# Layer 1 of a four-layer convolution chain: the negated row maxima reach all partitions by a DRAM write and read

## The chip, the core and the metric

The kernel runs on one core of a Trainium2 chip, in float32. The metric is device microseconds from the start to the end of one execution; the number given for a kernel is the median of its runs. A profile is one execution of its own, taken by the hardware profiler.

## The reference

Four layers follow each other on an input of 4 images x 192 channels x 64 x 64. Layer 0 is a deformable convolution with channel attention and an MLP, layer 2 is windowed attention with an MLP, layer 3 is a dynamic depthwise convolution. The change is in layer 1, a non-local block over all 4096 positions of an image:

```python
g_x = _conv1x1(x, g_w, g_b).reshape(B, O, N)            # O = 96, N = 4096
theta_x = _conv1x1(x, theta_w, theta_b).reshape(B, O, N)
phi_x = _conv1x1(x, phi_w, phi_b).reshape(B, O, N)
f1 = jnp.einsum('bon,bom->bnm', theta_x, phi_x)
f_div_C = jax.nn.softmax(f1, axis=-1)
y = jnp.einsum('bnm,bom->bon', f_div_C, g_x)
return _conv1x1(y.reshape(B, O, H, W), W_w, W_b) + x
```

The softmax of a query runs over all 4096 keys, and its maximum is taken off before the exponential.

## The kernel before

One program handles the four images (b = 0 to 3) in turn: layer 1, layer 2's windows, then the rest of layers 2 and 3. Layer 0 of the next image is spread over them. Its gather (an indirect DMA per tap and unit of 128 pixels into `ring`, blends on ACT and DVE into `row` and `xo`, matmuls `h`) is woven into layer 1 of images 0 to 2: `beside(k + 1)` in `layer1` emits some two and a half taps a step. Each unit of that gather also loads its centre pixels, `ti` (L584), with two DMAs on SP's queue into one of three buffers. Image 3 has no next image, so its layer 1 is alone.

Keys lie on the partitions and queries along the free dimension. `keys` makes `ph` (phi) and `gx` (g, with a column of ones for the softmax's sum). `layer1` goes through 16 chunks of 256 queries (QN), and for each through 8 groups (NG) of 4 x 128 keys (G). A step k is one group of one chunk:

- `load(i)` (L928 to L933): a chunk's x comes by DMA into `xc` (SP's queue, but ACT's for the first two chunks of images 1 and 2; four buffers); a matmul and an ACT copy make theta, `ths`.
- `score(i, g)` (L939 to L946): four score matmuls of 128 keys x 256 queries into PSUM (two buffers), an ACT copy of the 128 x 1024 block to a slot in SBUF, and a DVE maximum into `top`. There are 10 slots in images 0 to 2 and 16 in image 3.
- `negated_max(i)`, once per chunk: two more DVE maxima (L951, L952) bring `top` down to 128 x 256. Two TensorE transposes (`mt`, L955) put queries on the partitions, and a DVE reduction with negation (`nm`, L957) leaves 128 x 2 numbers: query 128 j + p in row p, column j. The next step needs them along the free dimension and the same on every partition. So DVE scales the identity by each column (`dg`, L960), TensorE multiplies that by a matrix of ones (`mb`, L963), and ACT copies the product to SBUF (`mbs`, L965), which is 128 x 256.
- for a step k of the main loop: DVE adds `mbs` to the slot (L1002), ACT takes the exponential (L1003), and TensorE adds the product with `gx` to `y` (L1005). After a chunk's last group, `y` is copied (L1011), and `finish` (L971 to L981) divides by the sum, applies W, adds x, and writes back to DRAM from SP's queue (L981).

A float32 matmul appears in the profile as two matmul records, so the two `mb` matmuls of a chunk are four records.

PSUM tag "a" has one buffer; `th`, `mt`, `mb`, `pd` and `wy` take it in turn. In the program, step k also emits the scores of step k + 10 (images 0 to 2) or k + 16 (image 3), and a chunk's `negated_max` follows its eighth score group. The order on each engine and queue isn't the program's order: a planner (the tile framework's scheduler) places each instruction by its readiness and its place in the program, and puts semaphore waits where one engine needs another or a buffer. The queues of SP, ACT and POOL then issue in that fixed order, and an instruction that waits holds all behind it on its engine.

Of the kernel before, what the change touches and what calls it, by code (L numbers as in the profile page):

```python
# [10 lines left out]
F32 = mybir.dt.float32  # L11
# [39 lines left out]
QN, G, EXTRA = 256, 4, 2  # L51
# [29 lines left out]
def conv_seq_kernel(ctx: ExitStack, tc: tile.TileContext, a, out: bass.AP):  # L81
    nc = tc.nc

    def pool_of(**kw):

        return tc.tile_pool(**({} if kw.get("space") == DRAM else {"reuse_waits": "tile"}), **kw)
# [4 lines left out]
    dram = ctx.enter_context(pool_of(name="tables", bufs=1, space=DRAM))  # L91
# [241 lines left out]

    xn_flat = [dram.tile([C, XNW], F32, tag=f"xnd{i}", name=f"xnd{i}") for i in range(2)]
    x_flat = [dram.tile([C, HW], F32, tag=f"xd{i}", name=f"xd{i}") for i in range(2)]
    xn_drams, x_drams = ([t.rearrange("(k p) n -> p k n", p=P) for t in ts] for ts in (xn_flat, x_flat))

    def variances(pv, sq, mean):
# [559 lines left out]
    def layer1(b, kv, beside):  # L898

        ph, gx = kv  # L900
        with ExitStack() as s:
            keep = s.enter_context(pool_of(name="l1", bufs=1))
            sb = s.enter_context(pool_of(name="l1a", bufs=2))
# [44 lines left out]
            def negated_max(i):  # L948

                top = tops.pop(i)  # L950
                nc.vector.tensor_tensor(top[:, 0:2], top[:, 0:2], top[:, 2:4], ALU.max)  # L951
                nc.vector.tensor_tensor(top[:, 0], top[:, 0], top[:, 1], ALU.max)  # L952
                pt = ps1.tile([128, 2, 128], F32, tag="a", name=f"mt_{b}_{i}")
                for j in range(2):
                    nc.tensor.transpose(pt[:, j, :], top[:, 0, bass.ts(j, 128)], ident)  # L955
                nm = sb.tile([128, 2], F32, tag="nm", name=f"nm_{b}_{i}")
                nc.vector.tensor_reduce(nm, pt, AX.X, ALU.max, negate=True)  # L957
                dg = sb.tile([128, 2, 128], F32, tag="dg", name=f"dg_{b}_{i}")
                for j in range(2):
                    nc.vector.tensor_scalar_mul(dg[:, j, :], ident, nm[:, j : j + 1])  # L960
                pb = ps1.tile([128, 2, 128], F32, tag="a", name=f"mb_{b}_{i}")
                for j in range(2):
                    nc.tensor.matmul(pb[:, j, :], lhsT=ones, rhs=dg[:, j, :], start=True, stop=True)  # L963
                mb = sb.tile([128, QN], F32, tag="mb", name=f"mbs_{b}_{i}")
                nc.scalar.copy(mb, pb.rearrange("p j n -> p (j n)"))  # L965
                return mb

# [18 lines left out]
            def next_scores(k):  # L986
                if k < NQ * NG:
                    i, g = divmod(k, NG)
                    if g == 0:
                        load(i)  # L990
                    score(i, g)
                    if g == NG - 1:
                        mbs[i] = negated_max(i)
# [3 lines left out]
            for k in range(NQ * NG):  # L997
                i, g = divmod(k, NG)
# [878 lines left out]
    with ExitStack() as s:  # L1877
        sb = s.enter_context(pool_of(name="l0first", bufs=1))
# [14 lines left out]
    with ExitStack() as s:  # L1893
        sb, pool = (s.enter_context(pool_of(name=n, bufs=1)) for n in ("norms0", "l0d0"))
# [4 lines left out]
    for b in range(B):  # L1899
        with ExitStack() as s:  # L1900
            sb = s.enter_context(pool_of(name="l1x", bufs=1))
# [36 lines left out]
        held = [oi]  # L1938
# [77 lines left out]
```

## Time and profile before

| | |
|---|---|
| median of 14 runs | 6950.65 us |
| lowest of the runs | 6923.98 us |
| profiled execution: its own time | 6973.63 us |
| profiled execution: span of the trace | 6971.9 us |
| granted TensorE clock, mean | 0.936 |
| busy: PE, PEld | 6270.0 us (90%), 4235.7 us (61%) |
| busy: DVE, ACT, POOL | 4791.0 us (69%), 3705.0 us (53%), 2038.0 us (29%) |
| chain that ended last | PE 60%, DVE 19%, ACT 7%, issue 5%, DMA 3% |

PE is TensorE's matmuls, PEld its weight loads (they overlap), DVE the vector engine, ACT the scalar engine, POOL GpSimd, SP the engine whose queue issues most DMAs. In the page, a line such as PE or DVE with 40 digits gives the busy share in tenths of 40 equal slices of the span, some 174 us each; DMA is the mean busy share of the 16 DMA engines. The chain is followed back from the last instruction through what released each step. In a timeline line stand the start in us, the duration in us, the engine, the source line, the operation, the tiles written and read, and the shapes; "x4" are four instructions of one kind merged, and brackets give the engine's idle time ahead and what ended it. SPq marks the issue of a DMA. In the windows view each engine has its busy us and its number of instructions in a stretch, then come the mean granted clock, the DMA engines' busy share and GB/s.

Layer 1's loops lie at about 915 to 1590, 2550 to 3230, 4190 to 4870 and 5735 to 6235 us.

### The profile page before, as it was taken

What the parts mean: (1) busy time and instruction counts of PE and PEld (TensorE: products, weight loads), DVE (VectorE), ACT (ScalarE), POOL (GpSimd) and SP (SyncE); (2) the same over time, 40 slices, a digit from 0 to 9 for tenths busy, and PEclk for the clock granted to TensorE, in tenths of its full rate; (3) what the DMA queues carried; (4) which work ended last, traced back from release to release, by engine and by line L of the source; (5) the groups of instructions that cost most, each with busy time, mean ns of one, the idle gap of its engine ahead of it and who ended that gap; (6) DMA issues with size and microseconds to landing.
All of it is one profiled execution on the core that took longest, in us unless ns stands there. A gap on an engine that the chain in (4) does not pass through costs nothing.

```text
span 6971.9 us, 116124 instructions
## 1 busy us (share of the span) xinstructions
PE 6270.0 (90%) x45392; PEld 4235.7 (61%) x45392; DVE 4791.0 (69%) x7011; ACT 3705.0 (53%) x6134; POOL 2038.0 (29%) x2276
## 2 busy tenths in 40 slices
PE   8787999999988899999988899999998889999876
PEld 4445578886643467887654457878564357776432
DVE  3654179985577758995676848987567767765656
ACT  3664268874544357884544337876444425545331
POOL 3663057642200036761210016763210000012100
PEclk8789989999989999999989999999999989999988
DMA  6784246651000166662010056764100010010000
GB/s 189 259 289 147 78 157 220 210 166 34 23 26 14 60 188 198 216 210 79 11 33 22 17 154 191 225 202 138 35 24 29 14 52 10 14 36 12 7 3 20
DMA packets 330499, 699.39 MB, mean 100 GB/s; under 512 B 60077, under 2 KB 217181, under 8 KB 329182
## 3 DMA queue, kind: packets, MB, share of 16 engines
q0 software_dynamic: 92736, 455.22, 20.0%
q1 hardware_dynamic: 236382, 235.95, 11.8%
q8 instruction: 358, 5.87, 0.3%
q14 instruction: 191, 1.56, 0.1%
q10 hardware_dynamic: 832, 0.79, 0.0%
HBM read 611.25 MB, written 78.87 MB: 99 GB/s over the span
## 4 chain that ended last, share of the span: by engine, by line
PE 60%; DVE 19%; ACT 7%; issue 5%; DMA 3%; another core or an unknown queue 1%; POOL 1%; SPq 0%; DVEq 0%; POOLq 0%; ACTq 0%
PE s L939 10%; PE y L1005 9%; PE h L608 6%; PE v L1170 2%; PE qk L1095 2%; DVE ha L1347 2%; PE h L1547 2%; PE qk L1096 2%; DVE ga L1347 2%; PE po L496 2%; PE t L1178 1%; PE h L821 1%; DVE top L946 1%; DVE row L597 1%; PE zm L1558 1%
## 5 line engine op out<-in xcount | busy, mean ns | idle before, releaser
L590 POOL DMA_INDIRECT ring<-table,idx x1152 | 1608.9, 1397 | 1178.8 <-issue 268.4
L939 PE MATMUL s<-ths,ph 96*128 96x256 f32 x4096 | 994.6, 390 | 21.6 <-ACT ths L933 12.8
L939 PEld LDWEIGHTS s<-ths,ph 96*128 96x128 f32 x4096 | 794.1, 195 | 165.4 <-ACT ths L933 21.4
L596 ACT ACTIVATE row<-ring,pos 128x384 f32<-128x384 f32 x1152 | 674.9, 609 | 219.3 <-DVE xo L601 122.4
L597 DVE SCALAR_TENSOR_TENSOR row<-ring,fr,row 128x384 f32<-128x384 f32 x1152 | 674.8, 612 | 100.5 <-ACT row L596 69.0
L1005 PE MATMUL y<-sc,gx 128*97 128x256 f32 x3008 | 721.6, 380 | 0.0
L1005 PEld LDWEIGHTS y<-sc,gx 128*97 128x97 f32 x3008 | 489.5, 164 | 126.9 <-issue 2.3
L600 ACT ACTIVATE xo<-row,pos 128x192 f32<-128x192 f32 x1152 | 489.1, 449 | 132.3 <-remote 50.9
L601 DVE SCALAR_TENSOR_TENSOR xo<-row,fr,xo 128x192 f32<-128x192 f32 x1152 | 449.6, 411 | 103.5 <-ACT xo L600 67.3
L941 ACT COPY sc<-s 128x1024 f32<-128x1024 f32 x376 | 378.0, 1005 | 193.1 <-PE s L939 168.3
L1002 DVE TENSOR_TENSOR sc<-sc,mbs 128x1024 f32<-128x1024 f32 x376 | 447.1, 1218 | 37.9 <-issue 20.7
L608 PE MATMUL h<-ti,xo 128*128 128x192 f32 x2304 | 456.6, 333 | 5.6 <-DVE xo L601 5.2
L946 DVE TENSOR_TENSOR top<-top,sc 128x1024 f32<-128x1024 f32 x282 | 344.5, 1222 | 163.2 <-ACT sc L941 133.3
L608 PEld LDWEIGHTS h<-ti,xo 128*128 128x128 f32 x2304 | 399.3, 194 | 42.3 <-DVE xo L601 12.0
L1003 ACT ACTIVATE sc<-sc 128x1024 f32<-128x1024 f32 x376 | 393.1, 1054 | 32.1 <-DVE sc L1002 25.2
L1154 DVE TENSOR_REDUCE es<-ex 128x6 f32<-128x384 f32 x264 | 133.3, 546 | 361.7 <-ACT ex L1150 361.7
L608 PE MATMUL h<-kept,xo 128*128 128x192 f32 x960 | 254.5, 403 | 112.9 <-DVE xo L601 71.0
L1588 POOL COPY gate<-gate 128x192 f32<-128x192 f32 x12 | 4.2, 351 | 1116.2 <-ACT gate L1581 1116.2
L608 PEld LDWEIGHTS h<-kept,xo 128*128 128x128 f32 x960 | 185.1, 226 | 202.9 <-DVE xo L601 104.8
L1347 DVE SCALAR_TENSOR_TENSOR ga<-gate,v,ga 128x1024 f32<-128x1024 f32 x234 | 299.7, 1281 | 7.2
L1005 PE MATMUL y<-se,gx 128*97 128x256 f32 x1088 | 260.4, 379 | 0.5 <-ACT yn L1011 0.5
L1552 ACT ACTIVATE z<-h,bias_fc1T 128x512 f32<-128x512 f32 x192 | 118.0, 687 | 227.2 <-PE h L1549 226.9
(392 smaller groups left out, 11573.3 us busy)
## 6 DMA issues: line engine op xcount, KB each, us to landing
ti<-table SPq DMA_DIRECT2D x768, 48.0 KB
ring<-table,idx POOLq DMA_INDIRECT x1152
xnd<-xn SPq DMA_DIRECT2D x4, 3270.0 KB
xi<-in_x_dram SPq DMA_DIRECT2D x32, 384.0 KB
xk<-xd SPq DMA_DIRECT2D x32, 384.0 KB
xd<-xc SPq DMA_DIRECT2D x64, 192.0 KB
table<-tt SPq DMA_DIRECT2D x32, 384.0 KB
xc<-xd SPq DMA_DIRECT2D x60, 192.0 KB
```

Source lines behind the costliest of these rows:

```text
L590: nc.gpsimd.indirect_dma_start(out=gt.rearrange("p q r c -> p (q r c)"), out_offset=None, in_=corners, in_offset=bass.IndirectOffsetOnAxis ...
L596: nc.scalar.activation(row, gt[:, 0], AF.Copy, scale=pos[:, t, 9 + tap : 10 + tap])
L597: nc.vector.scalar_tensor_tensor(row, gt[:, 1], fr[:, t, 9 + tap : 10 + tap], row, ALU.mult, ALU.add)
L600: nc.scalar.activation(xo[:, j, :], row[:, 0, :], AF.Copy, scale=pos[:, t, tap : tap + 1])
L601: nc.vector.scalar_tensor_tensor(xo[:, j, :], row[:, 1, :], fr[:, t, tap : tap + 1], xo[:, j, :], ALU.mult, ALU.add)
L608: nc.tensor.matmul(acc[m // 2][:, bass.ts(m % 2, C)], lhsT=xo.rearrange("p j c -> p (j c)")[:, bass.ts(m, 128)], rhs=tt, start=t == 0 and ...
L939: nc.tensor.matmul(p[:, t, :], lhsT=ph[:, bass.ts(G * g + t, 128)], rhs=ths[i], start=True, stop=True)
L946: nc.vector.tensor_tensor(tops[i], tops[i], to, ALU.max)
L1002: nc.vector.tensor_tensor(ex, ex, mbs[i].unsqueeze(1).to_broadcast([128, G, QN]), ALU.add)
L1003: nc.scalar.activation(ex, ex, AF.Exp)
L1005: nc.tensor.matmul(py, lhsT=gx[:, G * g + t, :], rhs=ex[:, t, :], start=g == 0 and t == 0, stop=g == NG - 1 and t == G - 1,)
L1347: nc.vector.scalar_tensor_tensor(acc[:, b], src(tap, b), w[:, tap : tap + 1], acc[:, b], ALU.mult, ALU.add)
```

## The change

For every chunk but the first of an image (60 of 64), `nm` is written to a DRAM tile of 256 numbers from SP's queue, in the order of the queries, and a second DMA on the same queue reads those 256 numbers into `mb` on all 128 partitions. Two DRAM tiles alternate. `dg`, the two matmuls with `ones` and ACT's copy remain for the first chunk of each image; `dg` has one buffer instead of two. Nothing else is touched.

```diff
+    max_dram = [dram.tile([QN], F32, tag=f"maxd{i}", name=f"maxd{i}") for i in range(2)]
...
                 nm = sb.tile([128, 2], F32, tag="nm", name=f"nm_{b}_{i}")
                 nc.vector.tensor_reduce(nm, pt, AX.X, ALU.max, negate=True)
-                dg = sb.tile([128, 2, 128], F32, tag="dg", name=f"dg_{b}_{i}")
+                mb = sb.tile([128, QN], F32, tag="mb", name=f"mbs_{b}_{i}")
+                if i > 0:
+                    held = max_dram[i % 2]
+                    nc.sync.dma_start(out=held.rearrange("(j p) -> p j", p=128), in_=nm)
+                    nc.sync.dma_start(out=mb, in_=held.unsqueeze(0).to_broadcast([128, QN]))
+                    return mb
+                dg = sb.tile([128, 2, 128], F32, tag="dg", name=f"dg_{b}_{i}", bufs=1)
                 for j in range(2):
                     nc.vector.tensor_scalar_mul(dg[:, j, :], ident, nm[:, j : j + 1])
                 pb = ps1.tile([128, 2, 128], F32, tag="a", name=f"mb_{b}_{i}")
                 for j in range(2):
                     nc.tensor.matmul(pb[:, j, :], lhsT=ones, rhs=dg[:, j, :], start=True, stop=True)
-                mb = sb.tile([128, QN], F32, tag="mb", name=f"mbs_{b}_{i}")
                 nc.scalar.copy(mb, pb.rearrange("p j n -> p (j n)"))
                 return mb
```

## The prediction

> **What bounds the kernel now.** I read the page first: its slices, then the chain of work that ended last.
>
> ```profile
> PE   8787999999988899999988899999998889999876
> DVE  3654179985577758995676848987567767765656
> DMA  6784246651000166662010056764100010010000
> PE s L939 10%; PE y L1005 9%; PE h L608 6%; PE v L1170 2%; PE qk L1095 2%; DVE ha L1347 2%; PE h L1547 2%; PE qk L1096 2%; DVE ga L1347 2%; PE po L496 2%; PE t L1178 1%; PE h L821 1%; DVE top L946 1%; DVE row L597 1%; PE zm L1558 1%
> ```
>
> Layer 1's loop fills slices 7 to 9, 16 to 18 and 25 to 27 (images 0 to 2, with the next image's gather beside it; DMA shows 5 to 7 there) and 34 to 36 (image 3, alone; DMA 0 or 1). PE shows 8 and 9 in them, DVE 8 and 9 in the first three. The two costliest lines of the chain, L939 and L1005, are its score and output matmuls. So I read single chunks of queries in the windows view: an undisturbed one of image 2, one of image 2 with a stall, one of image 3.
>
> ```profile
> core 0: us, PE busy (x) PEld busy (x) DVE busy (x) ACT busy (x) POOL busy (x), PEclk, DMA share, GB/s
> 4449.26:4490.49 41.23, 41.23 (x206) 34.53 (x205) 39.24 (x65) 35.14 (x62) 33.70 (x21) 1.00 0.73 229
> 4618.00:4667.00 49.00, 45.84 (x205) 37.40 (x204) 39.59 (x64) 35.63 (x60) 30.11 (x23) 0.90 0.64 204
> 5854.50:5885.70 31.20, 31.05 (x146) 24.61 (x144) 22.36 (x25) 16.67 (x19) 0.00 (x0) 1.00 0.04 13
> ```
>
> In the undisturbed chunk PE is busy for 41.23 of 41.23 us, at full clock, with DVE at 39.24. In image 3 it is 31.05 of 31.20. PE is the bound of both; DVE comes close in images 0 to 2. The stalled chunk takes 49 us at a mean clock of 0.90: an idle PE is paid twice. Next the tile view of `mb`, who waited for it:
>
> ```profile
>   ACT mbs L965: 92.2, 22
>   DVE sc L1002: 17.0, 14
>   PEld th L931: 14.3, 6
> ```
>
> Then the timeline across one undisturbed chunk boundary (chunk 5 of image 2), which shows what the maxima gate:
>
> ```profile
> 4409.62 0.42 DVE L957 TENSOR_REDUCE nm<-mt 128x2 f32<-128x256 f32 x1
> 4410.28 0.47 DVE L960 TENSOR_SCALAR dg<-ident,nm 128x128 f32<-128x128 f32 x2
> 4410.72 0.68 PE L963 MATMUL mb<-dg,ones 128*128 128x128 f32 x4
> 4411.64 0.35 ACT L965 COPY mbs<-mb 128x256 f32<-128x256 f32 x1
> 4412.39 2.35 DVE L1002 TENSOR_TENSOR sc<-sc,mbs 128x1024 f32<-128x1024 f32 x2
> 4413.86 1.04 ACT L1003 ACTIVATE sc<-sc 128x1024 f32<-128x1024 f32 x1
> 4414.01 3.72 PE L939 MATMUL s<-ths,ph 96*128 96x256 f32 x16
> 4417.57 1.89 PE L1005 MATMUL y<-sc,gx 128*97 128x256 f32 x8
> ```
>
> `nm` ends at 4410.04, `mbs` at 4411.99, the first addition starts 0.40 us later, and the chunk's first output matmuls (L1005 on `sc`) start at 4417.57. By program order `mbs` is wanted three steps after it is made; in the trace it is wanted at once: at each `nm` the additions of all earlier chunks are done (I counted 8n additions before the n-th `nm` in every image), and PE has at most one step (8 matmuls) of the previous chunk left in images 0 to 2. What PE has to do across the boundary is that rest, `th`, two score groups (3.72 us) and some gather matmuls. They fill it just to 4417.57.
>
> **Removed, on 60 of the 64 chunks.** PE: four matmuls `mb`. In the boundary shown the next output matmul follows 0.51 us after `mb`'s start, in image 3 it is 0.44 us, which is what PE gets back: 45 x 0.51 + 15 x 0.44 = 30 us. DVE: two `dg`, 0.47 us a chunk, 28 us; ACT: one copy of 0.37 us, 22 us. DVE and ACT are not the bound, so I count only PE's 30 us. The PSUM slot "a" is now free after `nm` and not after `mbs`, so `th` can start about 2 us earlier; the order of PE's work changes by it, its amount doesn't. I price it at nothing; PE being full across the boundary hides it.
>
> **Added.** Two DMAs on SP's queue, the second waiting for the first to land. The trace has no such pair for 1 KB, but it has one of the same kind: the write of x back (L981) and the load (L928) that waits for that write. Quiet (image 3), then beside the gather (image 1):
>
> ```profile
> 5870.17 0.30 SPq L981 DMA_DIRECT2D xd<-xc  x1
> 5872.30 0.30 SPq L928 DMA_DIRECT2D xc<-xd  x1
> ```
>
> ```profile
> 2795.13 0.31 SPq L981 DMA_DIRECT2D xd<-xc  x1
> 2797.68 2.36 SPq L584 DMA_DIRECT2D ti<-table  x4
> 2800.09 0.58 SPq L928 DMA_DIRECT2D xc<-xd  x1
> ```
>
> Quiet, the dependent read is issued 2.13 us after the write. Beside the gather it is 4.96 us; the other pairs that I looked at in image 1 have 3.83 to 4.73. The last packet of the quiet read ends 1.87 us after its issue by the trace's packets, beside the gather at 2.96 to 3.41 (medians by image). Both rows move 192 packets of 1 KB, the new read 128 of 1 KB, the new write 256 of 4 bytes, if each element is a packet. Packets of 4 bytes take 9 ns and of 1 KB 46 ns here, so the data is nothing: 16 x 9 and 8 x 46 ns on each engine. From `nm`'s end to `mbs` ready the bounds are 2.13 + 1.87 = 4.0 us and 4.96 + 3.41 = 8.4 us, against 1.69 (image 3) and 1.95 us (image 2) now. For image 3 I take 4.0, it has no gather. For images 0 to 2 the DMA engines are busy 0.73 of the time, so the loaded rows are nearer; the pair is smaller than they are, and I take 6.4.
>
> The Trainium skill, DMA: Bandwidth & Descriptors, section Anatomy of one DMA, speaks against the change: it puts a fixed cost of about 2.0 us on each DMA, most of it the receipt of the write. By that rule a pair would be 4 us in every image, and the sum would be the first rival's. The quiet row agrees (2.13 us); the loaded one doesn't.
>
> **Images 0 to 2.** After `mbs` comes an addition (1.2 us), an exponential (1.05) and about 0.3 of semaphores before PE can start: 6.4 + 2.55 = 8.95 us after `nm`. PE is there without `mb` at 7.53 - 0.51 = 7.0. So PE waits some 1.95 us a chunk: 45 x 1.95 = 88 us. With 4.0 us it is nothing, with 8.4 us 3.95 a chunk.
>
> The clock: after PE's pause of 3.6 us before 1300.9 the windows view has 0.50 for 3.4 us, then 1.00; after one of 2.8 us near 4623 the trace's clock is 0.50 for 10.2 us; after one of 2.1 us near 1344.7 it stays at 1.00. At 3.4 us a half clock costs 1.7 us; on half of the chunks, 45 x 0.5 x 1.7 = 38 us. The Trainium skill, TensorE: Matmul & The Clock Gate, section Part 1: The HAM clock gate, has a free-running window of about 3.4 us, which fits why pauses near 2 to 3 us sometimes halve it.
>
> Against that: PE already pauses by 2 us or more near `nm` in some 15 of the 45 chunks, at matmuls whose wait is for a `ti` load. There the new wait lies in the same pause: 15 x 1.95 = 29 us off.
>
> Behind the write and the read on SP stand the `ti` loads (two per unit of gather) and the `xc` load. SP is held from its arrival at the write until `nm`, and again until the write has landed. `ti` is three buffers deep: by the trace it is issued 5.3 us (lower quartile) to 8.0 us (median) before PE waits for it, and its semaphore is complete 3.6 us after issue (median; 5.0 at 95%). In the boundary shown SP has nothing to issue from 4410.91 to 4414.13, since it waits for PE; the hold mostly lies in there. I price it at nothing, cover gone it is up to 2 us a chunk, 90 us. `xc` is issued tens of us ahead. Behind the waiting addition on DVE stand gather blends for which PE waits later; that is in the wait priced above.
>
> **Image 3.** 4.0 us is 2.3 later than now. Its first output matmul comes 26.5 us after `nm`, since PE has some six steps of output matmuls in hand. The additions behind it shift; if the order on ACT kept the exponentials ahead of the score copies that empty PSUM, PE would lose up to 2.3 x 15 = 35 us. The planner's order goes by when inputs and buffers are ready (it has put the load L928 just behind the write that frees its buffer, some 13 steps ahead of its place in the program), so I take 0.
>
> **The sum:** -30 + 88 + 38 - 29 = +67 us, on the profiled execution's 6973.6 us: 7041. That execution is 23 us over the median of the runs shown (6950.65); on that scale it is 7018.
>
> **Rivals.**
> *Covered* (faster): the pair lands within 4.45 us of `nm` (7.0 - 2.55), or the planner puts enough gather matmuls ahead of the chunk's first output matmul. Then PE's 30 us come back: 6921, and to some 6905 if the earlier `th` ends some of the pauses. For: the quiet row, the small data, DVE and ACT with less to do. Against: DMA 0.73 busy, and 4.96 us in the same image's neighbours. The point that decides is 4.45 us.
> *A wash*: about 5.1 us, 0.65 us a chunk, 29 us that cancel the 30: 6950.
> *Loaded, and SP held*: 8.4 us, 3.95 x 45 = 178, half clock in every chunk 77, less 15 x 3.95 = 59 and 30: +166, 7117; with some late `ti` loads up to 7170. For: pauses of 2 to 5 us on late `ti` are there already.
>
> **How the numbers follow.** About 0.2%, 14 us, is what a measurement of this kernel can tell from no change. Forecast (+20 to +120 us) 0.45, covered 0.25, wash 0.10, loaded 0.20. The forecast's own range is 6970 to 7070. The range has to reach into the covered case and most of the loaded one: 6908 to 7160. Faster 0.25, same 0.10, slower 0.65.
>
> **What would show it.** In the changed profile: the lines of `dg`, `mb` and the copy left for four chunks only; SP showing the write and read per chunk with 3 to 5 us between; DVE's L1002 waiting on a DMA of `mbs`; in undisturbed chunks of images 0 to 2 a PE pause before the first output matmul and a period above 41.2 us, with more stretches at 0.50 clock; image 3's period at 30.8. I am wrong if those periods are 40.7: then the pair was covered; and wrong in the place if image 3 grows, or if `ti` waits grow more than the one on `mbs`.

## The result: 7649.5 us, 10% slower, and the profile after

The changed kernel takes 7649.5 us (median of 10 runs, 7618.78 to 7700.17). Before, measured beside it, takes 6950.66; the ratio is 1.101, with a 95% interval of 1.099 to 1.104. The forecast was 7018 and its range ended at 7160: the sign was right, the size ten times too small (699 us against 67). The profiled execution spans 7676.0 us (before 6971.9) at a mean granted clock of 0.896 (0.936). Lines shift: `nm` is L958, the write `maxd` L962, the read `mbs` L963, the score copy L942, `top` L947, the addition L1008, the exponential L1009, the output matmul L1011, and in `finish` `yn` L980, `wy` L985.

The page's slices, its granted clock, and its chain by line:

```profile
PE   7779977789987987878988888778998898888886
DVE  4653376665677566765586747676567755555656
PEclk8889888889999998989999998889999979889998
DMA  6782355651000365663010155655100010001000
PE y L1011 3%; PE s L940 3%; DMA maxd<-nm 2%; DMA mbs<-maxd 2%; PE v L1176 1%; PE qk L1101 1%; PE h L1553 1%; PE qk L1102 1%; DVE ga L1353 1%; PE t L1184 1%; PE ht L1344 1%; DVE ha L1353 1%; PE h L609 1%; PE zm L1564 1%; DVE top L947 1%
```

The two new DMAs stand in the chain, which before had DMA at 3% in all; the chain that the page could follow covers 38% of the span. Layer 1's four loops in the windows view (from the first `nm` of an image to its last), and under them one chunk of image 2 and one of image 3:

```profile
core 0: us, PE busy (x) PEld busy (x) DVE busy (x) ACT busy (x) POOL busy (x), PEclk, DMA share, GB/s
906.70:1748.30 841.60, 668.53 (x3051) 551.50 (x3050) 572.78 (x892) 511.49 (x842) 384.09 (x275) 0.88 0.57 155
2728.40:3559.30 830.90, 660.42 (x3050) 545.93 (x3050) 572.38 (x891) 511.70 (x842) 394.35 (x276) 0.89 0.58 158
4547.80:5382.20 834.40, 665.71 (x3050) 549.17 (x3050) 572.20 (x892) 511.10 (x842) 388.39 (x275) 0.88 0.58 157
6304.40:6895.40 591.00, 486.02 (x2047) 375.47 (x2048) 327.53 (x326) 251.75 (x271) 1.29 (x2) 0.89 0.05 13
...
4923.10:4978.10 55.00, 42.61 (x201) 35.31 (x200) 39.63 (x64) 34.72 (x59) 31.31 (x26) 0.88 0.73 207
6486.31:6527.22 40.91, 33.18 (x141) 25.54 (x140) 22.10 (x23) 16.76 (x18) 0.00 (x0) 0.87 0.05 13
```

The same loops in before took 658.7, 662.0, 660.7 and 461.7 us:

```profile
914.60:1573.30 658.70, 636.84 (x3106) 534.30 (x3106) 575.27 (x919) 509.54 (x856) 415.43 (x275) 0.98 0.62 195
2551.80:3213.80 662.00, 637.78 (x3106) 533.74 (x3106) 575.48 (x921) 510.06 (x856) 417.20 (x277) 0.98 0.62 196
4190.80:4851.50 660.70, 637.81 (x3106) 534.59 (x3106) 575.00 (x920) 509.19 (x856) 421.61 (x276) 0.98 0.62 196
5737.40:6199.10 461.70, 457.90 (x2104) 363.20 (x2105) 331.74 (x354) 250.51 (x285) 1.29 (x2) 0.99 0.04 13
```

They grow by 183, 169, 174 and 129, in sum 655 of the span's 704 us. Of the other 49, 36 lie between the end of image 2's loop and the start of image 3's (922 us against 886); in the traces of other runs below, which leave that stretch as it is, it takes 872 to 915 us, so it isn't shown that the change made them. PE's idle time in the loops of images 0 to 2 goes from 69 to 512 us, its busy time, at a lower clock, from 1912 to 1995. In image 3 idle goes from 4 to 105, busy from 458 to 486. So of the 655 us, 544 are idle PE and 110 are longer busy time. Since the `mb` matmuls are gone (30 us by the prediction's price) and the rest of PE's work is the same, the lower clock costs some 140 us by this estimate.

Who waited for the read, by its line, and the timeline of a chunk boundary (chunk 8 of image 2):

```profile
  DVE sc L1008: 530.6, 43
  DVE se L1008: 185.4, 16
```

```profile
4922.68 0.42 DVE L958 TENSOR_REDUCE nm<-mt 128x2 f32<-128x256 f32 x1
4923.12 0.38 SPq L962 DMA_DIRECT2D maxd<-nm  x1
4929.79 1.46 PE L940 MATMUL s<-ths,ph 96*128 96x256 f32 x6
4931.68 0.35 SPq L963 DMA_DIRECT2D mbs<-maxd  x1
4932.07 0.95 POOL L591 DMA_INDIRECT ring<-table,idx  x1 [0.30 <-DMA ring<-table,idx]
4932.14 4.66 SPq L585 DMA_DIRECT2D ti<-table  x4
...
4941.27 2.36 DVE L1008 TENSOR_TENSOR sc<-sc,mbs 128x1024 f32<-128x1024 f32 x2 [12.84 <-DMA mbs<-maxd]
4943.64 3.73 PE L1011 MATMUL y<-sc,gx 128*97 128x256 f32 x8 [12.39 <-ACT sc L1009]
4947.83 1.22 POOL L591 DMA_INDIRECT ring<-table,idx  x1 [11.03 <-DVE row L598]
```

The write is issued 0.02 us after `nm` ends; 8.56 us later it has landed and the read is issued; 9.59 us after that DVE can add. PE ran out of work at 4931.25 and stands for 12.39 us. The gather stands with it, because its blends are queued on DVE behind the waiting addition: the POOL row at the end waited 11.03 us for one of them. Over chunks 1 to 15 (medians by image) the read is issued 8.6 to 9.0 us after the write and the addition starts 7.0 to 7.9 after the read, 16.8 to 17.5 after `nm`; the first output matmul follows at 19.3 to 20.0. A chunk takes 55.2 us. In image 3 the two steps are 7.85 and 4.73 us, the addition starts at 12.5, and a chunk takes 40.8.

So the first question is why the pair takes 12.5 us on quiet DMA queues and 17 beside the gather, where I had taken 4.0 and 6.4.

### The profile page after: what moved, and what is told of

Same layout as the page of the kernel before. It is cut to its first block, busy times and chain, and to the rows that moved or that the text cites. A ratio compares the mean times of both kernels' runs of the same rounds, so it can differ in the third digit from the quotient of the medians.

```text
span 7676.0 us, 115523 instructions
## 1 busy us (share of the span) xinstructions
PE 6401.9 (83%) x45152; PEld 4305.8 (56%) x45152; DVE 4775.4 (62%) x6891; ACT 3709.7 (48%) x6074; POOL 1946.9 (25%) x2276
## 3 DMA queue, kind: packets, MB, share of 16 engines
q14 instruction: 190, 1.56, 0.1%
## 5 line engine op out<-in xcount | busy, mean ns | idle before, releaser
L591 POOL DMA_INDIRECT ring<-table,idx x1152 | 1521.4, 1321 | 1753.6 <-DVE row L598 789.0
L940 PE MATMUL s<-ths,ph 96*128 96x256 f32 x4096 | 1019.8, 395 | 33.1 <-issue 13.1
L1011 PE MATMUL y<-sc,gx 128*97 128x256 f32 x3008 | 790.4, 405 | 307.4 <-ACT sc L1009 307.4
L940 PEld LDWEIGHTS s<-ths,ph 96*128 96x128 f32 x4096 | 809.0, 199 | 188.5 <-issue 26.5
L1011 PEld LDWEIGHTS y<-sc,gx 128*97 128x97 f32 x3008 | 521.6, 176 | 466.7 <-ACT sc L1009 319.0
L1008 DVE TENSOR_TENSOR sc<-sc,mbs 128x1024 f32<-128x1024 f32 x376 | 450.6, 1217 | 532.3 <-DMA mbs<-maxd 530.6
L1009 ACT ACTIVATE sc<-sc 128x1024 f32<-128x1024 f32 x376 | 392.7, 1053 | 444.6 <-DVE sc L1008 441.4
L942 ACT COPY sc<-s 128x1024 f32<-128x1024 f32 x376 | 378.4, 1006 | 277.1 <-PE s L940 213.3
L609 PEld LDWEIGHTS h<-ti,xo 128*128 128x128 f32 x2304 | 408.3, 198 | 41.9 <-issue 11.8
L947 DVE TENSOR_TENSOR top<-top,sc 128x1024 f32<-128x1024 f32 x282 | 344.5, 1222 | 125.1 <-ACT sc L942 105.4
L1011 PE MATMUL y<-se,gx 128*97 128x256 f32 x1088 | 292.1, 412 | 89.8 <-ACT se L1009 80.4
L1008 DVE TENSOR_TENSOR se<-se,mbs 128x1024 f32<-128x1024 f32 x136 | 162.3, 1218 | 195.1 <-DMA mbs<-maxd 185.4
```

What stands on the lines that cost most here:

```text
L591: nc.gpsimd.indirect_dma_start(out=gt.rearrange("p q r c -> p (q r c)"), out_offset=None, in_=corners, in_offset=bass.IndirectOffsetOnAxis ...
L609: nc.tensor.matmul(acc[m // 2][:, bass.ts(m % 2, C)], lhsT=xo.rearrange("p j c -> p (j c)")[:, bass.ts(m, 128)], rhs=tt, start=t == 0 and ...
L940: nc.tensor.matmul(p[:, t, :], lhsT=ph[:, bass.ts(G * g + t, 128)], rhs=ths[i], start=True, stop=True)
L947: nc.vector.tensor_tensor(tops[i], tops[i], to, ALU.max)
L1008: nc.vector.tensor_tensor(ex, ex, mbs[i].unsqueeze(1).to_broadcast([128, G, QN]), ALU.add)
L1009: nc.scalar.activation(ex, ex, AF.Exp)
```

## What the pair costs by itself

Ratios are to before on the same chip, beside the kernel named; before takes 6818 to 6972 us, by chip.

First a kernel of DMAs alone: a write from SBUF to DRAM, a read of it back on the same queue, and a DVE copy that waits for the read, each form eight times.

```diff
+for to, of, back, read in forms:
+    nc.sync.dma_start(out=to, in_=of)
+    nc.sync.dma_start(out=back, in_=read)
+    nc.vector.tensor_copy(src, dst)
+# one.rearrange("(j p) -> p j", p=128) <- src[:, 0:2]   the change's write: 256 pieces of 4 B in one row of 1 KB
+# near[:, 0].rearrange("(j p) -> p j", p=128) <- the same, near is [256, 16]: pieces 64 B apart
+# lines[:, 0]... <- the same, lines is [256, 128]: pieces 512 B apart
```

> Only the DMAs, one after the other in a chain on a quiet chip (each write waits for the last read's copy on DVE, each read for its write); none of the four layers is computed. Eight times each: 256, 128 or 32 pieces of 4 bytes into one 1 KB row, 256 pieces of 4 bytes each into a 512-byte line of its own or at 64 bytes' distance, 128 pieces of 8 bytes, 2 of 512 bytes, 128 of 1 KB; then a read of 128 x 1 KB from one 1 KB row, or from 128 rows. Theory 1, the pieces cost: a write of 256 x 4 bytes lands in some 7.8 us, 128 x 8 and 128 x 4 in 4 to 5, 32 x 4 near 2.5, 2 x 512 and 128 x 1 KB near 2; if what counts is that the pieces share one line, then 256 in lines of their own land near 2 to 3 us too. Rival, a write with a dependent read has a fixed price of 7.8 us whatever its shape: all of them 7 to 8. For the read: if the shared source row costs, one row read 128 times takes some 4.5 us and 128 rows some 2; otherwise both 2.

Medians of seven repeats, in us:

| write | write to dependent read | read | read to DVE |
|---|---|---|---|
| 256 x 4 B in one 1 KB row (the change) | 8.32 | the row, 128 times | 5.07 |
| 128 x 4 B in one 512 B row | 7.56 | the row, 128 times | 5.00 |
| 32 x 4 B in 128 B | 3.34 | 32 times | 5.32 |
| 128 x 8 B in one 1 KB row | 3.16 | the row, 128 times | 4.25 |
| 2 x 512 B, the same row | 1.10 | the row, 128 times | 2.96 |
| 256 x 4 B, 64 B apart | 1.59 | 128 rows of 64 B | 1.69 |
| 256 x 4 B, 512 B apart | 1.56 | 128 rows of 512 B | 1.86 |
| 128 x 1 KB | 1.70 | 128 rows of 1 KB | 2.12 |
| 128 x 1 KB | 1.70 | one of them, 128 times | 3.02 |

The timeline of this kernel for the change's own form, for the same 256 pieces 64 B apart, and for two pieces of 512 B:

```profile
68.12 0.37 SPq L58 DMA_DIRECT2D one<-src  x1
76.28 0.32 SPq L59 DMA_DIRECT2D dst<-one  x1
81.35 0.29 DVE L60 COPY src<-dst 128x256 f32<-128x256 f32 x1 [13.25 <-DMA dst<-one]
...
461.06 0.37 SPq L58 DMA_DIRECT2D near<-src  x1
462.65 0.32 SPq L59 DMA_DIRECT2D dst<-near  x1
464.34 0.29 DVE L60 COPY src<-dst 128x256 f32<-128x256 f32 x1 [3.30 <-DMA dst<-near]
...
222.89 0.24 SPq L58 DMA_DIRECT2D one<-src  x1
223.99 0.32 SPq L59 DMA_DIRECT2D dst<-one  x1
226.94 0.29 DVE L60 COPY src<-dst 128x256 f32<-128x256 f32 x1 [4.08 <-DMA dst<-one]
```

The change's pair takes 13.4 us with nothing beside it. It isn't the number of pieces: 256 of them 64 B apart land in 1.59 us. It isn't a fixed price either: the same 1 KB in two pieces lands in 1.10. What is slow is pieces that lie closer together than 64 B; where between 8 and 64 B the cost ends wasn't tried. Distance isn't all of it, and three rows are off what was expected: 128 pieces of 4 B take 7.56 us (4 to 5 expected), 128 of 8 B 3.16 (4 to 5) and 32 of 4 B 3.34 (near 2.5). No rule for these three is shown. The trace shows the same thing from the other side: in quiet image 3 the packets of a write are over 1.1 us after its issue (median), 9 ns each, and still the write lands at 7.85. Time of packets doesn't say when a write has landed.

The read costs too: one row to 128 partitions takes 0.9 us more than 128 rows (3.02 against 2.12), and just after a write in small pieces 1.3 to 2 us more again (4.25 to 5.07, where it is 2.96 after two pieces).

## Smaller doses of the same wait

If the landing is the cause, a write in larger pieces has to shorten every chunk by what it lands earlier. First `nm` turned by TensorE to two rows of 128, so that two pieces of 512 B are written:

```diff
+                    pr = ps1.tile([2, 128], F32, tag="a", name=f"nr_{b}_{i}")
+                    nc.tensor.transpose(pr, nm, ident)
+                    row = sb.tile([2, 128], F32, tag="nmrow", name=f"nmrow_{b}_{i}")
+                    nc.vector.tensor_copy(row, pr)
-                    nc.sync.dma_start(out=held.rearrange("(j p) -> p j", p=128), in_=nm)
+                    nc.sync.dma_start(out=held.rearrange("(j p) -> j p", p=128), in_=row)
```

> The changed kernel, but nm is turned on TensorE into two rows of 128 and copied to SBUF by DVE, and the write is 2 pieces of 512 bytes; the read is the same. Theory 1, the 256 pieces of 4 bytes make the write land late: from write to read some 2.1 us quiet and 3 to 5 beside the gather, mbs ready 6 to 7 us earlier less some 1 us for the turn, the additions at about +7.5 us (image 3) and +11 us (images 0 to 2) after nm; time about 6950 + 150 to 350 us. Rival, any dependent pair costs this: 7600 to 7720.

7046.12 us against 6824.76 for before on the same chip, ratio 1.033 (1.028 to 1.039). Then pieces of 8 B, with the additions reading the maxima in the order in which they then lie:

```diff
-                    nc.sync.dma_start(out=held.rearrange("(j p) -> p j", p=128), in_=nm)
+                    nc.sync.dma_start(out=held.rearrange("(p j) -> p j", p=128), in_=nm)
...
-                nc.vector.tensor_tensor(ex, ex, mbs[i].unsqueeze(1).to_broadcast([128, G, QN]), ALU.add)
+                # ex and mbs[i] both viewed as q t j p, mbs[i] from "q (p j)"
```

> The changed kernel, but nm is written in its own order, 128 pieces of 8 bytes, and the additions read the columns in that order (step 2). Theory 1, the price goes by the number of pieces: write to read 4 to 5 us instead of 7.8 to 9, time some 200 to 300 us under the changed kernel, if DVE reads a step of 2 at the same rate. Rival, it is fixed: no gain, 7600 to 7720.

7258.32 us on that chip, ratio 1.068 (1.061 to 1.076); the addition takes 1218 ns as before. Beside the gather this write takes 5.8 to 6.0 us to land, where 4 to 5 was expected. One pair of the 512 B kernel (chunk 4 of image 2), and the addition that waits for it:

```profile
4403.54 0.44 SPq L966 DMA_DIRECT2D maxd<-nmrow  x1
4407.49 0.34 SPq L967 DMA_DIRECT2D mbs<-maxd  x1
...
4413.15 2.36 DVE L1012 TENSOR_TENSOR sc<-sc,mbs 128x1024 f32<-128x1024 f32 x2 [4.85 <-DMA mbs<-maxd]
```

Beside the gather this write takes 3.4 to 3.9 us to land (1.10 quiet), and its read 5.7 (3.16 quiet). The write is near the prediction's loaded rows (3.83 to 4.96), the read isn't (2.96 to 3.41): it is one row for 128 partitions, and the prediction had counted its reads to the last packet, which in the kernel of DMAs comes 0.4 us before DVE starts. So even this pair takes 9.0 to 9.6 us, more than the prediction's upper bound of 8.4. With the changed kernel (profiled on another chip) they make a series, in us from `nm`'s end, chunks 1 to 15:

| | addition, images 0-2 | first output matmul | period | the prediction's formula | addition, image 3 | period |
|---|---|---|---|---|---|---|
| 2 x 512 B | 10.4 | 13.0 | 47.6 | 48.4 | 5.1 | 30.9 |
| 128 x 8 B | 14.1 | 16.4 | 51.2 | 51.8 | 7.4 | 34.7 |
| 256 x 4 B | 16.9 | 19.5 | 55.2 | 54.9 | 12.5 | 40.8 |

The formula is the prediction's own: 41.2 less 0.5 for `mb`, plus the first output matmul's time less 7.0, plus 1.7 for the half clock. It holds to within 0.8 us for all three. So in images 0 to 2 the chain of steps was right, and the time that went into it wrong. In image 3 nothing is lost at 5.1 us, and beyond it 1.2 to 1.7 us for each us: 3.8 between 5.1 and 7.4, 6.1 between 7.4 and 12.5. There my price was a zero, and the cause is another one.

## Image 3: not the lateness, but what is queued behind it

The change in image 3 alone:

```diff
-                if i > 0:
+                if i > 0 and beside is None:
```

> The change in image 3 alone; images 0 to 2 keep the on-chip path. Theory: in the changed kernel image 3's loop took 591 us instead of 462 because DVE's queue stands at the first addition until mbs has landed, 12.5 us after nm; behind it waits the multiplication that finishes the previous chunk (L980 of the changed kernel), and PE waits for that although it has output matmuls of its own in hand. So +120 to +140 us here. Rival, image 3 lost time only as an after-effect of images 0 to 2 or by the planner's other order: under +40 us.

6950.5 us against 6818.85 on the same chip, ratio 1.022 (1.019 to 1.025): +132 us, in step with the 129 of the changed kernel's fourth loop. Image 3's first output matmul of a chunk comes 26.5 us after `nm` in before, and the maxima are now there after 12.5. There is time enough for them, and PE still stands for 7.7 us a chunk. My first theory was that DVE's queue is what stands. So I moved image 3's additions to GpSimd, which has nothing else there, in before as a control and in the kernel with the change in image 3:

```diff
-                nc.vector.tensor_tensor(ex, ex, mbs[i]..., ALU.add)
+                by = nc.gpsimd if beside is None else nc.vector
+                by.tensor_tensor(ex, ex, mbs[i]..., ALU.add)
```

> The kernel before with image 3's additions of mbs on GpSimd instead of DVE (no write or read); the control for the next. If GpSimd takes under 3.5 us for one addition of 128 x 1024, its eight fit into the 31.2 us of a chunk and the time is within 30 us of before; slower additions would show as a longer period of image 3.

> As e5_image3, the change in image 3 alone, but image 3's additions are on GpSimd, so GpSimd waits for mbs and DVE doesn't. Theory, what costs is what stands behind the wait in DVE's queue: the write and read then cost at most 20 us over e8_pool_before instead of some 130. Rival, the late mbs itself (the slots that come free late, the exponentials) starves PE: +100 us or more over e8_pool_before.

Both missed. The control takes 6943.71 us (1.020, 1.018 to 1.022), since its image 3 period is 38.2 by itself, and with the change 7071.38 (1.039, 1.036 to 1.042), period 47.7: 128 us more, as if nothing had been moved. The waits of the second kernel say where the hold went:

```profile
POOL se L1009 <- DMA mbs<-maxd: 205.7, 8, 26.6
POOL sc L1009 <- DMA mbs<-maxd: 177.6, 7, 26.5
ACT sc L1010 <- POOL sc L1009: 140.0, 64, 10.3
```

The exponentials (L1010) wait for the additions, and the score copies that empty PE's PSUM buffers are queued behind the exponentials on ACT. The wait had changed its engine only, so the run can't tell whether lateness or order costs the time. What sets the order is the planner, which puts an addition where it takes its maxima to be ready. The next pair left everything on its engine and changed the order alone: in image 3 each addition is queued on DVE behind the score maximum of step k + 11, some 15 us after `nm`, in before and with the change.

```diff
+                behind = newest.get(k + 11, newest.get(k + 10)) if beside is None else None   # newest[k]: the top of step k
+                if behind is not None:
+                    tc.add_manual_dep(added.ins, behind.ins.name, NoSync, reason="order")
```

> The way of before (dg, mb, copy), but in image 3 each addition (k) is queued on DVE behind the score maximum of step k+11: the planner may no longer put a chunk's additions straight behind nm. It is the control for the next run. PE's work and its hand of output matmuls stay, so both theories expect image 3's period within 31 to 32.5 us and the time within 30 us (0.4%) of before; first addition some 12 to 20 us after nm instead of 1.7, and nobody waits for it.

> The change in image 3 alone once more, on the chip of this call, one look for the trace beside the two ordered kernels. Period 40 to 41 us as before in this study, some +130 us.

> The change in image 3 alone, with the same order as the control (each addition of image 3 queued on DVE behind the score maximum of step k+11). Theory (it is the planner's order, which puts the waiting additions ahead of DVE's other work, that makes the late maxima cost PE anything): the pair lands 12 to 13 us after nm as before in this study, the addition is now queued later than that, DVE waits for it little or not at all, image 3's period falls from 40.8 to 31 to 32.5, PE idle below 1 us a chunk, and the time is within 25 us of the control (ratio 1.000 to 1.004), where the unordered change in image 3 cost 132 us. Rival (the lateness itself, or SP's hold on the x loads and the write back, costs it in any order): period stays at 36 to 41 and the time at +70 to +130 over the control.

On one chip, before at 6817.87: the control takes 6809.18 (0.999, 0.997 to 1.002), the change in image 3 without the order 6995.22 (one run; its image 3 loop is 605 us long, the control's 465), and with the order 6835.61 (1.002, 1.000 to 1.005). That is 26 us over the control, at the edge of what the theory allowed (25) and a fifth of the 132; 8 of them are one wait in the last chunk, which has no later maximum to be queued behind. The pair is no faster: write to read 8.52 us, read to addition 5.25, the addition starts 13.75 us after `nm`, against 8.40, 5.16 and 13.62 without the order. The windows of the two image 3 loops, without the order and with it, then the largest waits of each in its window that bear on this:

```profile
5602.00:6207.00 605.00, 484.23 (x2046) 374.27 (x2047) 327.52 (x326) 251.86 (x271) 1.29 (x2) 0.89 0.05 13
```

```profile
PE wy L985 <- DVE yn L980: 111.3, 13, 9.0
DVE sc L1008 <- DMA mbs<-maxd: 95.9, 7, 14.1
DVE se L1008 <- DMA mbs<-maxd: 95.2, 7, 13.7
```

```profile
5572.00:6047.00 475.00, 460.06 (x2059) 358.20 (x2060) 322.23 (x326) 254.78 (x271) 1.29 (x2) 0.98 0.06 16
```

```profile
DVE sc L1008 <- DMA mbs<-maxd: 15.9, 7, 13.2
DVE se L1008 <- DMA mbs<-maxd: 4.0, 7, 1.0
PE wy L985 <- DVE yn L980: 8.1, 1, 8.1
```

Without the order the first two additions stand straight behind `nm` in DVE's queue, and behind them the division `yn` of the chunk that is just done and the next chunk's maxima. PE, in its own fixed order, comes to `wy`, which needs `yn`, and stands with its output matmuls behind it. The boundary of the kernel without the order shows it:

```profile
5804.66 2.36 DVE L1008 TENSOR_TENSOR se<-se,mbs 128x1024 f32<-128x1024 f32 x2 [13.62 <-DMA mbs<-maxd]
5806.94 1.22 DVE L945 TENSOR_TENSOR top<-sc 128x1024 f32<-128x1024 f32 x1
5808.08 0.41 DVE L980 TENSOR_TENSOR yn<-yn,pd 96x256 f32<-96x256 f32 x1
```

With the order, `yn` and the maxima go first, and maxima that are 13.75 us late cost almost nothing. So in image 3 late maxima cost PE time only through what stands behind the wait: in the planner's order maxima that come after 12.5 us cost some 130 us, in the other order maxima that come after 13.75 us cost 26.

## SP's hold

The prediction priced SP's standing at nothing, up to 90 us with its cover gone. To see the pair without its wait, the way of before keeps its `dg`, `mb` and copy, and the pair goes into a tile that nobody reads:

```diff
+                if i > 0:
+                    spare = sb.tile([128, QN], F32, tag="spare", name=f"spare_{b}_{i}", bufs=1)
+                    nc.sync.dma_start(out=held.rearrange("(j p) -> p j", p=128), in_=nm)
+                    nc.sync.dma_start(out=spare, in_=held.unsqueeze(0).to_broadcast([128, QN]))
```

> The kernel before with its on-chip path for every chunk, and besides it the write and the read of the change into a tile that nothing reads. SP is held as in the changed kernel and the DMAs run, but no engine waits for them. Theory 1, the wait for mbs at DVE is the cost: within 0 to +60 us of the time before (some late ti loads). Rival, SP held for 8 us a chunk makes the ti loads late, and that is the cost: +300 to +600 us, most of it in images 0 to 2.

6962.57 us against 6824.76, ratio 1.021 (1.015 to 1.027): 138 us, over twice the upper end of what I had expected. The write without the read:

```diff
-                    nc.sync.dma_start(out=spare, in_=held.unsqueeze(0).to_broadcast([128, QN]))
```

> e2_unread without its read: the on-chip path for every chunk, and the write of nm, 256 pieces of 4 bytes, which no one waits for. SP stands for nm but not for the landing. e2_unread was 2.1% over before. If SP's hold until the write has landed made that, this is within 0.5% of before; if the 256 pieces or the altered order of the planner made it, it is 1.5 to 2.5% over as well.

6840.19 us against 6818.85 on another chip, 1.003 (1.001 to 1.005). With no read to wait for the landing, SP goes on at once. PE's waits on the gather's loads, with the unread pair, then with the write alone:

```profile
PE h L609 <- DMA ti<-table: 50.1, 19, 4.3
PE h L609 <- DMA xo<-table: 35.7, 9, 6.5
```

```profile
PE h L609 <- DMA xo<-table: 19.5, 10, 4.8
```

The theory was that the late `ti` loads behind SP's wait are the cost. To test it I gave `ti` six buffers instead of three, in before and with the unread pair, and ran the unread pair again beside them.

```diff
-                    tt = sb.tile([128, C], F32, tag="tt", name=f"ti_{b}_{t}_{taps[0]}")
+                    tt = sb.tile([128, C], F32, tag="tt", name=f"ti_{b}_{t}_{taps[0]}", bufs=6)
```

> The way of before, with the pair of DMAs into a tile that nobody reads, once more beside the next runs on one chip: 1.5 to 2.7% slower than before, as in its first run (2.1%); waits of PE on ti some 50 us in all.

> The same with six buffers for ti instead of three, so that a ti load is asked for earlier in SP's order. Theory (the unread pair costs because SP stands until the write has landed and the ti loads behind it come late): PE's waits on ti fall from 50 us to below 15 and the time to within 0.7% of before (and of the kernel with six buffers and no pair). Rival (the pair's packets or its place in the planner's order cost it): stays at 1.5 to 2.7%. If the planner doesn't ask earlier with six buffers, nothing moves, and this run says nothing.

> Before with six buffers for ti, the control of the run above. PE pauses now and then on late ti loads in before too, so 0 to 40 us faster (0 to 0.6%).

On this chip before takes 6971.85 us, the unread pair 7022.89 (1.007, 1.004 to 1.010), the same with six buffers 7037.36 (1.008, 1.006 to 1.011) and before with six buffers 6961.98 (0.998, 0.995 to 1.001). The first expectation is missed: the pair costs 51 us here, not 100 to 190. PE's waits on `ti` were 4.5 us in all on this chip, and with six buffers, which have a `ti` load issued some 24 us before its matmul instead of 10 (medians), there are none in the list of waits; the time didn't move. So the `ti` loads are not what costs the 51 us here. The list still has 31.1 us of waits on `xo<-table`, the centre pixels of the ninth tap, which come from the same line and queue and which six buffers leave alone. In order: before, the unread pair with six buffers, the changed kernel.

```profile
PE h L608 <- DMA xo<-table: 2.5, 4, 1.3
PE h L609 <- DMA xo<-table: 31.1, 10, 6.4
PE h L609 <- DMA xo<-table: 17.8, 8, 4.7
```

On the first chip 50.1 us on `ti` came with the larger cost, so they may be part of the difference there; that isn't shown, since no run there had more buffers.

The write also holds up its neighbours. In layer 1 of images 0 to 2 of the changed kernel, a packet of the gather's queue that starts while the 4-byte pieces land takes 634 ns in the mean and up to 9.1 us, against 242 ns away from the pair; while two pieces of 512 B land it takes 232 ns. With the write alone it takes 486 ns, and that kernel is only 21 us slower than before. So on these two chips, whose before takes 6825 and 6819 us, the larger part of the unread pair's 138 us comes with the read and SP's wait for it; the two were not separated.

It stays open why the cost differs between chips. A part may lie in before itself, whose chunks of images 0 to 2 are longer on the slower chip. Where the pair costs 51 us, they take 43.9 us in the mean without it (six buffers) and 45.4 with it. On a chip with before at 6818 us they take 41.9 without it (the ordered control, whose images 0 to 2 are before's), and on the chip where the pair costs 138 us 44.9 with it. In the changed kernel the term is mostly hidden: no wait of PE for `ti` is listed, and those for `xo<-table` grew by 15 us; its chunks have pauses of some 12 us in which the loads can land.

## Can before be bettered?

The experiments point at one thing to try on the old way: `mb` can be made straight from `nm`, its column broadcast as the weights and the identity as the other operand. That takes the two `dg` off the path.

```diff
-                    nc.vector.tensor_scalar_mul(dg[:, j, :], ident, nm[:, j : j + 1])
...
-                    nc.tensor.matmul(pb[:, j, :], lhsT=ones, rhs=dg[:, j, :], start=True, stop=True)
+                    nc.tensor.matmul(pb[:, j, :], lhsT=nm[:, j : j + 1].to_broadcast([128, 128]), rhs=ident, start=True, stop=True)
```

> The way of before without dg: mb = nm's column (broadcast along the free dimension as the weights) times the identity, so the two DVE scalings go and nothing else does. nm to mbs gets shorter by one dg and its semaphore, 0.5 to 0.9 us, in all 64 chunks. Theory A (before, PE has just enough to do across the boundary, so mbs earlier by under 1 us is worth nothing and DVE isn't the bound): within 15 us (0.2%) of before, either way. Theory B (the slope of one us per us that the later additions showed holds on this side too): 48 x 0.5 to 0.9 = 24 to 43 us faster, 0.35 to 0.6%.

> Before without dg (nm's column as the weights, the identity as the other operand) and with six buffers for ti: the two edits together, as a candidate that beats both kernels. Theory that before's remaining pauses are late ti loads: 20 to 50 us faster than before; rival (they are the gather's own rows): within 15 us.

Without `dg` 6808.74 us, ratio 0.999 (0.997 to 1.001), beside a before of 6817.87. The addition starts 1.54 us after `nm` instead of 2.63, and the first output matmul at 7.43 instead of 7.54 (images 0 to 2, against the ordered control on the same chip, which has the way of before there): maxima that come 1.1 us earlier are worth 0.1, since PE is busy up to there. With six buffers as well, on the last chip, 6947.79 against 6971.85, 0.998 (0.996 to 1.001). The 24 us are in the range that was hoped for, but neither kernel can be told from before, so no version here is shown to beat it. The first one's trace says that the boundary in before is PE's and not the maxima's, as the prediction had it.

## Why the prediction was right or wrong

**The bound, the deadline and the formula: right.** PE is the bound of undisturbed chunks, its work across a boundary reaches 7.0 us past `nm`, and each us beyond is paid. Three kernels meet the formula within 0.8 us a chunk, and the run without `dg` shows the other side of the deadline. Two terms inside it were off. The half clock was priced at 1.7 us a chunk; by the trace's clock PE works at half clock for 277 us in the three loops, against 74 before, so the loss is some 2.3 us a chunk (an estimate). And the pauses of before were put down to `ti` loads; with six buffers for `ti` before takes the same time (0.998), so that reading isn't borne out.

**The failed step is the size of the pair.** "Packets of 4 bytes take 9 ns and of 1 KB 46 ns here, so the data is nothing", and from it "the pair is smaller than they are, and I take 6.4". The write back of x and the load that waits for it were taken as bounds, 4.0 and 8.4 us. Neither half of the new pair lies within them. The write of 4-byte pieces side by side takes 8.32 us to land quiet and 8.6 to 9.0 beside the gather; the read of one row for 128 partitions just after it takes 5.07 and 7.0 to 7.9. The measured 17 us in the prediction's own sum: the first output matmul is at 19.5 instead of 8.95, so the wait is 45 x 12.5 = 563 and not 88; the half clock comes in every chunk, 77 and not 38; the existing pauses, 2.8 us a chunk before (a mean period of 44.0 against 41.2) and 0.5 after (55.7 against 55.2), give back 45 x 2.3 = 104 and not 29; PE's `mb` 23. That is +513, and the three loops grew by 526. It is no independent check, since the 104 is read off the measured periods and the half clock's 77 should be about 100. The prediction had written that the trace has no such pair and that the write would be 256 packets of 4 bytes where its rows have 192 of 1 KB; the right answer to that was a far wider upper end, not a value below the loaded row.

The Trainium skill's page DMA: Bandwidth & Descriptors, section Anatomy of one DMA, gives about 2.0 us as the fixed cost of a DMA on GpSimd's path; the prediction took it for DMAs on SP's queue. There the writes differ from it in both directions: 1.10 us for 2 x 512 B and 8.32 for 256 x 4 B. In its section Specifications the page says that below 512 B a DMA does a read-modify-write. That alone doesn't give the 8.32, since 256 pieces of 4 B at a distance of 64 B land in 1.59. The runs show what the distances cost, not the mechanism.

**Image 3 at 0: wrong, and wrong in the place, as its last sentence allowed.** It grew by 129 us. I had named a way of this kind, on another engine (ACT's exponentials ahead of the score copies, at most 35 us at 2.3 us of delay; the delay became 10.8), and then set it aside because the planner's "order goes by when inputs and buffers are ready". It can only go by when the planner takes them to be ready, and here the additions stood straight behind `nm` on DVE, some 12 us ahead of their data, with `yn` behind them, for which PE waited. The runs with the order pinned show this.

**SP's hold at 0: wrong by 51 us on one chip and up to 138 on another when the pair stands alone; in the changed kernel it is mostly covered.** PE's waits on `ti` didn't grow there, those on `xo<-table` by 15 us.

**The rivals.** *Covered* and *a wash* needed the pair within 4.45 or at 5.1 us of `nm`; only image 3's 512 B write comes near (5.1), and there it is indeed free. *Loaded, and SP held* had the right direction and ended at 8.4 us, for the same reason as the forecast.

## What to carry to other kernels

Price a DMA write by the shape of its pieces in DRAM before its bytes: a column written as 4-byte pieces side by side takes 8.3 us to land, turned to two rows first 1.1, and the time of its packets shows neither. Where a trace has no row of the same shape, its nearest rows are no bound. And where a fixed order stands on a planner's guess of a landing, look for what is queued behind the instruction that waits: moving image 3's additions behind the work that was ready took back four fifths of the loss, with the data just as late.

## What the hardware showed that I had not expected

- 256 pieces of 4 B: 8.32 us from the write's issue to its landing side by side, 1.59 at a distance of 64 B, 1.56 at 512 B. 32 pieces side by side still take 3.34.
- A row read on 128 partitions takes 3.02 us, 128 different rows 2.12; just after small pieces were written to it, 4.25 to 5.07.
- Beside the gather a write of two 512 B pieces lands in 3.4 to 3.9 us instead of 1.10, and the read behind it takes 5.7 instead of 3.16: the load adds 2.3 to 2.8 us to each step of that pair.
- While 256 pieces of 4 B land side by side, a packet of the gather takes 634 ns instead of 242 in the mean, and up to 9.1 us; beside two pieces of 512 B it takes 232.
